# Attention denominators by transposes and a free-dimension sum, with the recurrence's input kept in natural order

## The chip, the cores and the metric

The kernel runs on one core of a Trainium2 chip. The metric is the device time in microseconds (us) of one execution; of several executions the median is given. Five engines work side by side, each with its own queue[...]: PE (TensorE, matrix products; PEld is its weight load), DVE (VectorE), ACT (ScalarE), POOL (GpSimd) and SP (SyncE, which here issues the transfers). On-chip memory is SBUF; matrix products land in PSUM[...]. All data is float32.

## The reference

The input `x` has shape (4, 128, 64, 64): four batches, 128 channels, 4096 positions. Two layers follow each other. Cut to what matters:

```python
# layer 0: every position attends to all others, 64 channels inside
q, k, v = wq @ x, wk @ x, wv @ x                   # per batch, 64 x 4096
x = x + wo @ (softmax(k^T q) applied to v)

# layer 1: t = tokens of x, 4 x 4096 x 128
t = t + causal_attention(layernorm(t), Wq, Wk, Wv)
# layer 1, second half: batch norm over all tokens, then a recurrence in time
Wx = layernorm(t) @ W.T
Wx = (Wx - mean) * rsqrt(var + 1e-5) * gamma + beta
def step(y, wx_t):
    y = sigmoid(wx_t + y @ V.T)
    return y, y
_, ys = scan(step, zeros, Wx over the 4096 time steps)
t = t + ys
```

Each attention needs, for every query, the sum of its exponentials: the softmax denominator. The recurrence is sequential over 4096 steps in the reference.

## The kernel before

The kernel has a fast path and a general one behind a flag that the fast path computes. Only the fast path runs here. Keys lie on partitions and queries along the free dimension, in blocks of 512 queries (`BLK`), so the exponentials `p` are summed over keys in two moves: DVE adds them up elementwise over all key tiles (`dsum`, then `den`, 128 x 512), and the 128 partitions that remain are summed at the end of each block. There are 64 blocks: 2 layers, 4 batches, 8 blocks each.

```python
def project(layer, b, g, agg, den):
    dp = misc("den_ps")                              # one of two shared PSUM buffers
    for j in range(TPB):                             # TPB = 4
        nc.tensor.matmul(dp[:, j : j + 1], lhsT=den[:, ts(j, P)], rhs=ones, start=True, stop=True)
    rec = recs[:, layer, b, ts(g, TPB)]
    nc.vector.reciprocal(rec, dp[:, :TPB])
    op = misc("o_ps")
    for j in range(TPB):
        nc.tensor.matmul(op[:, ts(j, P)], lhsT=agg[:, ts(j, P)], rhs=wv1 if layer else wo2, ...)
    for j in range(TPB):
        t = xs[:, b, ds(g * BLK + j * P, P)]
        nc.vector.scalar_tensor_tensor(t, in0=op[:, ts(j, P)], scalar=rec[:, j : j + 1], in1=t, ...)
```

A product with the one-column `ones` puts the sums of 128 queries on 128 partitions, one per partition, as `rec` is needed there.

The recurrence is cut into `NCH` = 256 chunks of `STEPS` = 16 time steps, which run side by side: one instruction handles one step of all 256 chunks of a batch. Each chunk first runs `WARM` = 12 steps of the chunk ahead of it to reach its starting state; a count at the end compares these states with the true ones and feeds the flag. The input of the recurrence is stored so that the 32 chunks of a block of 512 lie side by side for each step:

```python
# in the last stage of a block of layer 1 (third())
wp = misc("wx_ps")
nc.tensor.matmul(wp, lhsT=wf, rhs=mem["xhT"], start=True, stop=True)
nc.vector.bn_stats(stats[:, b * NB + g], wp)
nc.scalar.copy(
    xs[:, b, ts(g, BLK)].rearrange("p (s c) -> p s c", c=CPB),     # CPB = 32
    wp.rearrange("p (c s) -> p s c", s=STEPS),
)
...
by_step = xs.rearrange("p b (g s c) -> p b s g c", s=STEPS, c=CPB)

def step(b, s):                                      # s from -12 to 15
    wx = by_step[:, b, s % STEPS]
    if s == -1:  y = start[:, b, 1:]
    elif s < 0:  y = yp.tile(...)
    else:        y = wx                              # the result takes the place of its input
    ps = ps_y.tile(...)
    nc.tensor.matmul(ps, lhsT=vf, rhs=prev[b], start=True, stop=True)
    z = yp.tile(...)                                 # the sum goes to SBUF
    nc.vector.scalar_tensor_tensor(z, in0=wx, scalar=scale, in1=ps, op0=ALU.mult, op1=ALU.add)
    nc.scalar.activation(y, z, AF.Sigmoid, bias=shift)
    prev[b] = start[:, b, :NCH] if s == -1 else y

def residual(b):                                     # after the last step of a batch
    for g in range(NB):                              # NB = 8
        engine = nc.vector if g < ON_DVE[b] else nc.gpsimd
        t = xr[:, b, ts(g, BLK)].rearrange("p (c s) -> p c s", s=STEPS)
        y = xs[:, b, ts(g, BLK)].rearrange("p (s c) -> p c s", c=CPB)
        engine.tensor_tensor(t, t, y, ALU.add)
    for h in range(2):
        nc.sync.dma_start(out=out[b, :, half], in_=xr[:, b, half])

ON_DVE = (0, 0, 4, 5)
pace = (1.40, 1.60, 1.75, 1.87)                      # order in which the batches' steps are written
```

`xr` holds the tokens before the recurrence; it is stored to memory as `x2` during the attention and loaded again at its end. The scheduler of the language may move instructions within a queue, so the written order isn't always the one that runs.

Of the kernel before, what the change touches and what calls it, by code (L numbers as in the profile page):

```python
# [9 lines left out]
F32 = mybir.dt.float32  # L10
AF = mybir.ActivationFunctionType
ALU = mybir.AluOpType
AX = mybir.AxisListType
PSUM = bass.MemoryType.PSUM

P = 128
BLK = 512
# [325 lines left out]
def fast_path(  # L343
# [20 lines left out]
    nc = tc.nc  # L364
    B, C, N = x.shape
    M = c_wqT.shape[1]
    assert C == P and M == P // 2 and N % CHUNK == 0
    NT = N // P
    NB = N // BLK
    TPB = BLK // P  # L370
    SHIFT = 32.0
    LOW, HIGH = 1e-25, 1e25
    WARM, TOL, STEPS = 12, 1e-6, 16
    NCH = N // STEPS
    CPB = BLK // STEPS

    const = ctx.enter_context(tc.tile_pool(name="const", bufs=1))
    xpool = ctx.enter_context(tc.tile_pool(name="x", bufs=1))
# [4 lines left out]
    xs = xpool.tile([P, B, N], F32, name="xs")  # L383
# [3 lines left out]
    def load(name, shape, *parts):  # L387
        t = const.tile(shape, F32, name=name)
        for dst, src in parts:
            nc.scalar.dma_start(out=dst(t), in_=src)  # L390
        return t
# [15 lines left out]
    vf = load("vf", [P, P], (whole, f_vT))  # L407
# [3 lines left out]
    ident = const.tile([P, P], F32, name="ident")  # L411
    make_identity(nc, ident)
    ones = const.tile([P, 1], F32, name="ones")
# [17 lines left out]
    with tc.tile_pool(name="batch", bufs=1) as batch, tc.tile_pool(name="rows", bufs=2) as rowp, tc.tile_pool(  # L431
        name="prob", bufs=4
    ) as prob, tc.tile_pool(name="work", bufs=2) as wk, tc.tile_pool(name="stat", bufs=4) as stat, tc.tile_pool(
        name="ps_s", bufs=2, space=PSUM
    ) as ps_s, tc.tile_pool(name="ps_a", bufs=2, space=PSUM) as ps_a, tc.tile_pool(
        name="ps_m", bufs=2, space=PSUM
    ) as ps_m:

        def misc(name):
            return ps_m.tile([P, BLK], F32, tag="m", name=name)  # L440
# [52 lines left out]
        def project(layer, b, g, agg, den):  # L493

            dp = misc("den_ps")
            for j in range(TPB):
                nc.tensor.matmul(dp[:, j : j + 1], lhsT=den[:, ts(j, P)], rhs=ones, start=True, stop=True)  # L497
            rec = recs[:, layer, b, ts(g, TPB)]
            nc.vector.reciprocal(rec, dp[:, :TPB])
            op = misc("o_ps")  # L500
            for j in range(TPB):
                nc.tensor.matmul(  # L502
                    op[:, ts(j, P)], lhsT=agg[:, ts(j, P)], rhs=wv1 if layer else wo2, start=True, stop=True
                )
            for j in range(TPB):
                t = xs[:, b, ds(g * BLK + j * P, P)]
                nc.vector.scalar_tensor_tensor(  # L507
                    t, in0=op[:, ts(j, P)], scalar=rec[:, j : j + 1], in1=t, op0=ALU.mult, op1=ALU.add
                )
# [37 lines left out]
        def finish1(b, g):  # L547
            agg, den = bs[b].agg, bs[b].den
            mem = {}

            def first():
                project(1, b, g, agg, den)
                mem["xh"] = wk.tile([P, TPB, P], F32, tag="xh2", name="xh2")
                normed(b, g, mem["xh"])

            def second():
                t = xs[:, b, ts(g, BLK)].rearrange("p (j c) -> p j c", c=P)
                xc = wk.tile([P, BLK], F32, tag="xc", name="xc")
                transposed(t, xc, "tT_ps", nc.scalar.copy)
                nc.sync.dma_start(out=x2[b, :, ts(g, BLK)], in_=xc)  # L560
                mem["xhT"] = wk.tile([P, BLK], F32, tag="xhT2", name="xhT2")
                transposed(mem["xh"], mem["xhT"], "xh2T_ps", nc.vector.tensor_copy)

            def third():
                wp = misc("wx_ps")
                nc.tensor.matmul(wp, lhsT=wf, rhs=mem["xhT"], start=True, stop=True)  # L566
                nc.vector.bn_stats(stats[:, b * NB + g], wp)

                nc.scalar.copy(
                    xs[:, b, ts(g, BLK)].rearrange("p (s c) -> p s c", c=CPB),  # L570
                    wp.rearrange("p (c s) -> p s c", s=STEPS),
                )

            yield 1, first
            yield 3, second
            yield 1, third
# [15 lines left out]
        for b in range(B):  # L592
            for g in range(NB):
                block(0, b, g, [((t, 0, BLK), (t + NT // 2, 0, BLK)) for t in range(NT // 2)])
            for g in range(NB):
                full = [((t, 0, BLK), (t + 1, 0, BLK)) for t in range(0, TPB * g, 2)]
                d = [(TPB * g + r, r * P, BLK - r * P) for r in range(TPB)]
# [150 lines left out]

    with tc.tile_pool(name="xr", bufs=1) as xrp, tc.tile_pool(name="y", bufs=2) as yp, tc.tile_pool(
        name="ps_y", bufs=2, space=PSUM
    ) as ps_y:
        xr = xrp.tile([P, B, N], F32, name="xr")
        for b in range(B):
            nc.sync.dma_start(out=xr[:, b], in_=x2[b])

        mv = xrp.tile([P, nc.vector.BN_AGGR_DIM], F32, name="mv")
        nc.vector.bn_aggr(mv, stats)
        scale = xrp.tile([P, 1], F32, name="scale")  # L760
        var = xrp.tile([P, 1], F32, name="var")
        nc.vector.tensor_scalar(var, mv[:, 1:2], BN_EPS, None, ALU.add)
        rsqrt(scale, var, xrp.tile([P, 1], F32, name="z"))
        nc.vector.tensor_tensor(scale, scale, gamma, ALU.mult)
        shift = xrp.tile([P, 1], F32, name="shift")
        nc.vector.tensor_tensor(shift, mv[:, 0:1], scale, ALU.mult)
        nc.vector.tensor_tensor(shift, beta, shift, ALU.subtract)

        by_step = xs.rearrange("p b (g s c) -> p b s g c", s=STEPS, c=CPB)
        start = xrp.tile([P, B, NCH + 1], F32, name="start")  # L770
        nc.gpsimd.memset(start[:, :, 0:1], 0.0)
        prev = [None] * B

        def step(b, s):

            grid = lambda t: t.rearrange("p (g c) -> p g c", c=CPB)
            wx = by_step[:, b, s % STEPS]
            if s == -1:
                y = grid(start[:, b, 1:])
            elif s < 0:  # L780
                y = grid(yp.tile([P, NCH], F32, tag=f"y{b}", name="y"))
            else:
                y = wx
            if prev[b] is None:
                nc.scalar.activation(y, wx, AF.Sigmoid, scale=scale, bias=shift)
            else:
                ps = grid(ps_y.tile([P, NCH], F32, tag=f"y{b}", name="y_ps"))
                nc.tensor.matmul(ps, lhsT=vf, rhs=prev[b], start=True, stop=True)  # L788
                z = grid(yp.tile([P, NCH], F32, tag=f"z{b}", name="z"))
                nc.vector.scalar_tensor_tensor(z, in0=wx, scalar=scale, in1=ps, op0=ALU.mult, op1=ALU.add)  # L790
                nc.scalar.activation(y, z, AF.Sigmoid, bias=shift)
            prev[b] = grid(start[:, b, :NCH]) if s == -1 else y

        def residual(b):

            for g in range(NB):
                engine = nc.vector if g < ON_DVE[b] else nc.gpsimd
                t = xr[:, b, ts(g, BLK)].rearrange("p (c s) -> p c s", s=STEPS)
                y = xs[:, b, ts(g, BLK)].rearrange("p (s c) -> p c s", c=CPB)
                engine.tensor_tensor(t, t, y, ALU.add)  # L800
            for h in range(2):
                half = slice(h * N // 2, (h + 1) * N // 2)
                nc.sync.dma_start(out=out[b, :, half], in_=xr[:, b, half])


        ON_DVE = (0, 0, 4, 5)
        pace = (1.40, 1.60, 1.75, 1.87)
        turns = [((s + WARM + 1) * pace[b], b, s) for b in range(B) for s in range(-WARM, STEPS)]
        for _, b, s in sorted(turns):
            step(b, s)  # L810
            if s == STEPS - 1:
                residual(b)


        count = xrp.tile([P, 2], F32, name="count")
        d = xrp.tile([P, B, NCH], F32, name="d")
        for b in range(B):
            grid = lambda t: t.rearrange("p (g c) -> p g c", c=CPB)
            nc.vector.tensor_tensor(grid(d[:, b]), by_step[:, b, STEPS - 1], grid(start[:, b, 1:]), ALU.subtract)
        nc.vector.tensor_tensor(d, d, d, ALU.mult)  # L820
        nc.vector.tensor_scalar(d, d, TOL * TOL, None, ALU.is_le)
        nc.vector.tensor_reduce(count[:, 0:1], d.rearrange("p b c -> p (b c)"), AX.X, ALU.add)

        r = recs.rearrange("p l b t -> p (l b t)")
        r2 = xrp.tile([P, 2 * B * NT], F32, name="r2")
        nc.vector.tensor_scalar(r2, r, LOW, None, ALU.is_ge)
        nc.vector.tensor_scalar(r, r, HIGH, None, ALU.is_le)
        nc.vector.tensor_tensor(r, r, r2, ALU.mult)
        nc.vector.tensor_reduce(count[:, 1:2], r, AX.X, ALU.add)
        total = xrp.tile([P, 1], F32, name="total")  # L830
        nc.vector.tensor_reduce(total, count, AX.X, ALU.add)
        tp = ps_y.tile([1, 1], F32, tag="y0", name="tp")
        nc.tensor.matmul(tp, lhsT=total, rhs=ones, start=True, stop=True)
        nc.vector.tensor_scalar(flag, tp, P * (B * NCH + 2 * B * NT) - 0.5, None, ALU.is_lt)


# [56 lines left out]
```

## Time and profile before

| What | Value |
|---|---|
| Time, median of 3 (lowest to highest) | 2267.13 us (2266.6 to 2267.83) |
| Span of the profiled execution | 2266.1 us |
| Mean granted TensorE clock | 0.987 |
| Recurrence, first activation to last | 2163.1 to 2215.2 us |
| Line 497, one-column products, PE passes | 512 of 246 ns |
| Line 497, weight loads | 512 of 191 ns |
| Line 499, reciprocal on DVE | 64 of 178 ns |
| Line 791, activation of the recurrence | 108 of 508 ns |
| Line 694, DVE add of 128 x 512, both inputs in SBUF | 64 of 692 ns |
| Line 800, residual add of 128 x 512 on POOL | 23 of 1917 ns |
| Line 800, the same on DVE | 9 of 2348 ns |

A row of the profile's groups gives the line, engine, operation, the tiles written and read with their shapes, the count, then busy time and mean duration, and what ended the idle time before it. The duration of an instruction overlaps with its neighbours', so a count times a mean can be more than the time that the engine took. The chain of waits follows the run back from its last instruction and so tells which work set the end.

### The profile page before, as it was taken

What the parts mean: (1) busy time and instruction counts of PE and PEld (TensorE: products, weight loads), DVE (VectorE), ACT (ScalarE), POOL (GpSimd) and SP (SyncE); (2) the same over time, 40 slices, a digit from 0 to 9 for tenths busy, and PEclk for the clock granted to TensorE, in tenths of its full rate; (3) what the DMA queues carried; (4) which work ended last, traced back from release to release, by engine and by line L of the source; (5) the groups of instructions that cost most, each with busy time, mean ns of one, the idle gap of its engine ahead of it and who ended that gap; (6) DMA issues with size and microseconds to landing.
All of it is one profiled execution on the core that took longest, in us unless ns stands there. A gap on an engine that the chain in (4) does not pass through costs nothing.

```text
span 2266.1 us, 31438 instructions
## 1 busy us (share of the span) xinstructions
PE 2185.7 (96%) x12764; PEld 1004.1 (44%) x12764; DVE 1440.8 (64%) x2684; ACT 1013.4 (45%) x1122; POOL 148.7 (7%) x230
## 2 busy tenths in 40 slices
PE   7999999999999999999999999999999999999980
PEld 3434355454333345544343435554434434544450
DVE  4877764444787774544678776444477876544486
ACT  4666623323666543333566552333366653333281
POOL 0000010000000000000000001000000001000007
PEclk9999999999999999999999999999999999999985
DMA  4000000000000000000000000000000000000033
GB/s 158 1 1 1 1 10 10 5 5 5 6 1 1 1 5 10 10 5 5 6 1 1 1 1 10 10 5 5 10 1 1 1 1 5 10 10 5 10 149 150
DMA packets 10536, 36.17 MB, mean 16 GB/s; under 512 B 1936, under 2 KB 2704, under 8 KB 8848
## 3 DMA queue, kind: packets, MB, share of 16 engines
q1 hardware_dynamic: 8640, 33.56, 3.8%
q8 instruction: 102, 1.67, 0.3%
q10 hardware_dynamic: 1744, 0.53, 0.1%
q14 instruction: 50, 0.41, 0.1%
HBM read 17.30 MB, written 16.78 MB: 15 GB/s over the span
## 4 chain that ended last, share of the span: by engine, by line
PE 92%; issue 3%; POOL 2%; DVE 2%; DMA 1%; ACT 0%; ACTq 0%; POOLq 0%; DVEq 0%
PE s_ps L620 20%; PE acc L679 20%; PE s_ps L611 20%; PE acc L671 19%; PE o_ps L502 3%; PE den_ps L497 2%; POOL xr L800 2%; PE r_ps L474 1%; PE wx_ps L566 1%; PE v_ps L469 1%; PE r_ps L488 1%; PE xhT_ps L531 1%; PE kc_ps L461 1%; PE xT_ps L483 1%; PE xh2T_ps L531 1%
## 5 line engine op out<-in xcount | busy, mean ns | idle before, releaser
L651 DVE TENSOR_TENSOR dsum<-dsum,p 128x1024 f32<-128x1024 f32 x676 | 827.7, 1224 | 507.6 <-ACT p L627 336.5
L625 ACT ACTIVATE p<-s_ps,nshift 128x1024 f32<-128x1024 f32 x512 | 570.9, 1115 | 380.2 <-PE s_ps L611 380.1
L627 ACT ACTIVATE p<-s_ps 128x1024 f32<-128x1024 f32 (+2 forms) x288 | 274.2, 952 | 632.6 <-PE s_ps L620 522.1
L611 PE MATMUL s_ps<-rows,kc 64*64 64x512 f32 x4096 | 538.6, 594 | 0.0
L671 PE MATMUL acc<-p,v 64*64 64x512 f32 x4096 | 535.2, 590 | 0.0
L620 PE MATMUL s_ps<-rows,xhT 128*128 128x512 f32 (+3 forms) x1152 | 504.9, 560 | 2.6 <-DVE rows L490 2.6
L679 PE MATMUL acc<-p,xh 128*128 128x512 f32 (+3 forms) x1152 | 501.6, 557 | 0.0
L679 PEld LDWEIGHTS acc<-p,xh 128*128 128x128 f32 x1152 | 215.9, 190 | 243.2 <-issue 234.7
L620 PEld LDWEIGHTS s_ps<-rows,xhT 128*128 128x128 f32 x1152 | 210.6, 190 | 229.0 <-issue 184.5
L671 PEld LDWEIGHTS acc<-p,v 64*64 64x64 f32 x4096 | 159.1, 133 | 279.9 <-issue 273.8
L611 PEld LDWEIGHTS s_ps<-rows,kc 64*64 64x64 f32 x4096 | 146.9, 133 | 248.2 <-issue 233.7
L425 POOL TENSOR_TENSOR ln_rstd<-ln_var,mhalf 128x4 f32<-128x4 f32 x64 | 66.7, 1042 | 1222.3 <-DVE ln_var L519 1211.5
L507 DVE SCALAR_TENSOR_TENSOR xs<-o_ps,recs,xs 128x128 f32<-128x128 f32 x256 | 73.0, 344 | 38.4 <-PE o_ps L502 38.4
L659 DVE TENSOR_TENSOR dsum<-dsum,p 128x256 f32<-128x256 f32 (+1 forms) x120 | 55.9, 496 | 64.2 <-POOL p L631 64.2
L631 POOL TENSOR_SCALAR_AFFINE_SELECT p<-p 128x128 f32<-128x128 f32 x128 | 34.5, 293 | 743.1 <-ACT p L627 743.1
L497 PEld LDWEIGHTS den_ps<-ones,den 128*128 128x128 f32 x512 | 64.6, 191 | 40.5 <-issue 20.5
L649 DVE COPY dsum<-p 128x1024 f32<-128x1024 f32 x60 | 41.4, 690 | 61.7 <-ACT p L627 55.4
L523 DVE TENSOR_SCALAR xh<-xs,ln_mv,ln_rstd 128x128 f32<-128x128 f32 x256 | 71.2, 341 | 1.9
L497 PE MATMUL den_ps<-ones,den 128*128 128x1 f32 x512 | 63.9, 246 | 0.0
L516 DVE BATCH_NORM_STATS2 ln_st<-xs 128x6 f32<-128x128 f32 x256 | 63.4, 269 | 0.0
L426 DVE TENSOR_TENSOR ln_z<-ln_rstd 128x4 f32<-128x4 f32 x64 | 10.5, 163 | 68.7 <-POOL ln_rstd L425 68.7
L790 DVE SCALAR_TENSOR_TENSOR z<-xs,scale,y_ps 128x256 f32<-128x256 f32 x108 | 48.5, 480 | 5.1 <-PE y_ps L788 4.5
(93 smaller groups left out, 1124.6 us busy)
## 6 DMA issues: line engine op xcount, KB each, us to landing
xs<-in_x SPq DMA_DIRECT2D x16, 512.0 KB, 7.8
x<-xc SPq DMA_DIRECT2D x32, 256.0 KB, 2.0
xr<-x SPq DMA_DIRECT2D x4, 2048.0 KB, 14.6
out_x<-xr SPq DMA_DIRECT2D x8, 1024.0 KB, 4.5
wk<-in_c_wkT ACTq DMA_DIRECT2D x2, 32.0 KB, 4.9
wo<-in_c_woT ACTq DMA_DIRECT2D x2, 32.0 KB, 4.3
wqT<-in_a_wqT ACTq DMA_DIRECT2D x1, 64.0 KB, 4.5
wkT<-in_a_wkT ACTq DMA_DIRECT2D x1, 64.0 KB, 5.8
```

The lines of the kernel that those rows point to most:

```text
L425: nc.gpsimd.tensor_tensor(y, var, mhalf[:, : y.shape[-1]], ALU.pow)
L497: nc.tensor.matmul(dp[:, j : j + 1], lhsT=den[:, ts(j, P)], rhs=ones, start=True, stop=True)
L502: nc.tensor.matmul(op[:, ts(j, P)], lhsT=agg[:, ts(j, P)], rhs=wv1 if layer else wo2, start=True, stop=True)
L507: nc.vector.scalar_tensor_tensor(t, in0=op[:, ts(j, P)], scalar=rec[:, j : j + 1], in1=t, op0=ALU.mult, op1=ALU.add)
L523: nc.vector.tensor_scalar(dst[:, j], xs[:, b, ds(g * BLK + j * P, P)], mv[:, j, 0:1], y[:, j : j + 1], ALU.subtract, ALU.mult)
L611: nc.tensor.matmul(ps[c * M : c * M + M, off : off + n], lhsT=bs[it.b].kc[part, ds(t % (NT // 2) * P + c * M, M)], rhs=rows[part], start=True,
L620: nc.tensor.matmul(ps[:, off : off + n], lhsT=lhsT, rhs=rhs, start=True, stop=True)
L625: nc.scalar.activation(it.p[:, :off], ps[:, :off], AF.Exp, bias=nshift)
L627: nc.scalar.activation(it.p[:, :off], ps[:, :off], AF.Exp, scale=float(P) ** -0.5)
L651: nc.vector.tensor_tensor(flat, flat, it.p, ALU.add)
L671: nc.tensor.matmul(bt.acc[r][h * M : h * M + M], lhsT=bt.v[part, t], rhs=it.p[part, o : o + n], start=it.first, stop=it.last,)
L679: nc.tensor.matmul(bt.acc[0][:, q0:], lhsT=bt.xh[:, t], rhs=it.p[:, o : o + n], start=it.first and h == 0, stop=it.last and h == 1,)
```

## The change

There are two parts. In the first, the partition sum of `den` is made by transposing its four 128 x 128 pieces on PE and adding along the free dimension with one DVE reduction. In the second, the recurrence's input is kept in the natural order of time, so a step reads every sixteenth element; the sums are written back to PSUM, from where ACT reads them; each step's result goes to a tile of its own and is added to the residual right after its step, on DVE when the step number divides by three and otherwise on POOL, and each batch's output is stored in one transfer. The first part is meant to replace products[...]; the second lets the residual run beside the recurrence and drops the permuted store.

```diff
             dp = misc("den_ps")
             for j in range(TPB):
-                nc.tensor.matmul(dp[:, j : j + 1], lhsT=den[:, ts(j, P)], rhs=ones, start=True, stop=True)
+                nc.tensor.transpose(dp[:, ts(j, P)], den[:, ts(j, P)], ident)
             rec = recs[:, layer, b, ts(g, TPB)]
-            nc.vector.reciprocal(rec, dp[:, :TPB])
+            nc.vector.tensor_reduce(rec, dp.rearrange("p (j k) -> p j k", k=P), AX.X, ALU.add)
+            nc.vector.reciprocal(rec, rec)
 ...
-                nc.scalar.copy(
-                    xs[:, b, ts(g, BLK)].rearrange("p (s c) -> p s c", c=CPB),
-                    wp.rearrange("p (c s) -> p s c", s=STEPS),
-                )
+                nc.scalar.copy(xs[:, b, ts(g, BLK)], wp)
 ...
-    tc.tile_pool(name="y", bufs=2) as yp
+    tc.tile_pool(name="y", bufs=3) as yp
 ...
-        by_step = xs.rearrange("p b (g s c) -> p b s g c", s=STEPS, c=CPB)
+        by_step = xs.rearrange("p b (c s) -> p b s c", s=STEPS)
+        ends = xrp.tile([P, B, NCH], F32, name="ends")
+        xr_by_step = xr.rearrange("p b (c s) -> p b s c", s=STEPS)
 ...
-                y = wx
+                y = ends[:, b] if s == STEPS - 1 else yp.tile(...)          # condensed
 ...
-                z = grid(yp.tile([P, NCH], F32, tag=f"z{b}", name="z"))
-                nc.vector.scalar_tensor_tensor(z, in0=wx, scalar=scale, in1=ps, op0=ALU.mult, op1=ALU.add)
-                nc.scalar.activation(y, z, AF.Sigmoid, bias=shift)
+                nc.vector.scalar_tensor_tensor(
+                    ps[:, :n], in0=wx, scalar=scale, in1=ps[:, :n], op0=ALU.mult, op1=ALU.add
+                )
+                nc.scalar.activation(y, ps[:, :n], AF.Sigmoid, bias=shift)
+            if s >= 0:
+                t = xr_by_step[:, b, s]
+                (nc.gpsimd if s % 3 else nc.vector).tensor_tensor(t, t, y, ALU.add)
+            if s == STEPS - 1:
+                nc.sync.dma_start(out=out[b], in_=xr[:, b])
-        def residual(b): ...                                                # removed, see above
```

In the warm-up a step now covers the 255 chunks that have one ahead of them (`n` = 255) in place of 256, and the check at the end compares the 255 states accordingly.

More of the change, by code (lines that the diff above doesn't have):

```diff
@@ L374, in fast_path @@
     NCH = N // STEPS
-    CPB = BLK // STEPS
     const = ctx.enter_context(tc.tile_pool(name="const", bufs=1))
@@ L744, in fast_path @@
         assert not waiting and not side
-    with tc.tile_pool(name="xr", bufs=1) as xrp, tc.tile_pool(name="y", bufs=2) as yp, tc.tile_pool(
+    with tc.tile_pool(name="xr", bufs=1) as xrp, tc.tile_pool(name="y", bufs=3) as yp, tc.tile_pool(
         name="ps_y", bufs=2, space=PSUM
@@ L767, in fast_path @@
         nc.vector.tensor_tensor(shift, beta, shift, ALU.subtract)
-        by_step = xs.rearrange("p b (g s c) -> p b s g c", s=STEPS, c=CPB)
-        start = xrp.tile([P, B, NCH + 1], F32, name="start")
+        by_step = xs.rearrange("p b (c s) -> p b s c", s=STEPS)
+        start = xrp.tile([P, B, NCH], F32, name="start")
         nc.gpsimd.memset(start[:, :, 0:1], 0.0)
+        ends = xrp.tile([P, B, NCH], F32, name="ends")
+        xr_by_step = xr.rearrange("p b (c s) -> p b s c", s=STEPS)
         prev = [None] * B
         def step(b, s):
-            grid = lambda t: t.rearrange("p (g c) -> p g c", c=CPB)
-            wx = by_step[:, b, s % STEPS]
+            wx = by_step[:, b, s] if s >= 0 else by_step[:, b, STEPS + s, : NCH - 1]
+            n = wx.shape[-1]
             if s == -1:
-                y = grid(start[:, b, 1:])
+                y = start[:, b, 1:]
             elif s < 0:
-                y = grid(yp.tile([P, NCH], F32, tag=f"y{b}", name="y"))
+                y = yp.tile([P, NCH - 1], F32, tag=f"y{b}", name="y")
+            elif s == STEPS - 1:
+                y = ends[:, b]
             else:
-                y = wx
+                y = yp.tile([P, NCH], F32, tag=f"y{b}", name="y")
             if prev[b] is None:
@@ L786, in step @@
             else:
-                ps = grid(ps_y.tile([P, NCH], F32, tag=f"y{b}", name="y_ps"))
-                nc.tensor.matmul(ps, lhsT=vf, rhs=prev[b], start=True, stop=True)
-                z = grid(yp.tile([P, NCH], F32, tag=f"z{b}", name="z"))
[L790 to L806, printed above, removed]
+                ps = ps_y.tile([P, NCH], F32, tag=f"y{b}", name="y_ps")
+                nc.tensor.matmul(ps[:, :n], lhsT=vf, rhs=prev[b], start=True, stop=True)
+                nc.vector.scalar_tensor_tensor(
+                    ps[:, :n], in0=wx, scalar=scale, in1=ps[:, :n], op0=ALU.mult, op1=ALU.add
+                )
+                nc.scalar.activation(y, ps[:, :n], AF.Sigmoid, bias=shift)
+            prev[b] = start[:, b] if s == -1 else y
+            if s >= 0:
[3 more added lines that the diff above has]
+                nc.sync.dma_start(out=out[b], in_=xr[:, b])
         pace = (1.40, 1.60, 1.75, 1.87)
@@ L810, in fast_path @@
             step(b, s)
-            if s == STEPS - 1:
-                residual(b)
         count = xrp.tile([P, 2], F32, name="count")
[L816 to L819, printed above, removed]
+        d = xrp.tile([P, B, NCH - 1], F32, name="d")
+        nc.vector.tensor_tensor(d, ends[:, :, : NCH - 1], start[:, :, 1:], ALU.subtract)
         nc.vector.tensor_tensor(d, d, d, ALU.mult)
@@ L833, in fast_path @@
         nc.tensor.matmul(tp, lhsT=total, rhs=ones, start=True, stop=True)
-        nc.vector.tensor_scalar(flag, tp, P * (B * NCH + 2 * B * NT) - 0.5, None, ALU.is_lt)
+        nc.vector.tensor_scalar(flag, tp, P * (B * (NCH - 1) + 2 * B * NT) - 0.5, None, ALU.is_lt)
 def kernel(
```

## The prediction

> **What bounds the kernel now.** I read the page first: busy shares, then the chain of waits.
>
> ```profile
> PE 2185.7 (96%) x12764; PEld 1004.1 (44%) x12764; DVE 1440.8 (64%) x2684; ACT 1013.4 (45%) x1122; POOL 148.7 (7%) x230
> ...
> PE 92%; issue 3%; POOL 2%; DVE 2%; DMA 1%; ACT 0%; ACTq 0%; POOLq 0%; DVEq 0%
> ```
>
> Both say TensorE. A busy PE alone proves little, because its ends are modelled; the chain confirms it, since it runs through PE work for 92% of the span. The PE rows of the waits list no wait over 1 us in the attention stage, and the busy table by stretch has PE at 2074.53 of 2080.00 us between 50 and 2130. There a TensorE saving counts in full, and 64% DVE leaves room. The change, though, also touches the last 100 us, where another order holds:
>
> ```profile
> 2190.00:2210.00 20.00, 20.00 (x90) 13.14 (x89) 19.72 (x45) 20.00 (x45) 0.00 (x0) 1.00 0.00 1
> 2210.00:2230.00 20.00, 4.66 (x21) 2.87 (x20) 19.95 (x20) 5.72 (x13) 15.52 (x8) 0.71 0.13 53
> 2230.00:2250.00 20.00, 0.19 (x2) 0.08 (x2) 17.54 (x11) 0.00 (x0) 20.00 (x11) 0.50 0.34 143
> ```
>
> Columns after the length: busy (count) of PE, PEld, DVE, ACT, POOL, then clock, DMA share, GB/s. The reader is to see two regimes: a recurrence (first row) in which POOL does nothing, and a residual stage in which PE and ACT do nothing. The timeline of that tail shows the same; first column start, second length:
>
> ```profile
> 2214.49 43.29 POOL L800 TENSOR_TENSOR xr<-xr,xs 128x512 f32<-128x512 f32 x23 [54.42 <-ACT xs L791]
> ...
> 2216.21 20.50 DVE L800 TENSOR_TENSOR xr<-xr,xs 128x512 f32<-128x512 f32 x9
> 2222.23 35.91 SPq L803 DMA_DIRECT2D out_x<-xr  x8
> ```
>
> So from 2214.5 the end is set by POOL's residual adds (to 2257.8) and then one 1 MB store.
>
> **Stage one, the denominators: what goes.** From the chain in order of time (start, length, what):
>
> ```profile
> 74.55 0.59 PE xhT_ps L531 x4
> ...
> 95.83 0.98 PE den_ps L497 x8
> 96.82 1.00 PE o_ps L502 x8
> 97.81 1.02 PE s_ps L611 x8
> ...
> 315.92 0.44 PE xhT_ps L531 x4
> ...
> 319.79 0.79 PE den_ps L497 x8
> ```
>
> Four products are eight PE passes (float32 goes in two), each with its own 128x128 weight load[...]. They hold the chain 0.98 us per block in layer 0 and 0.79 in layer 1: 32 x 0.98 + 32 x 0.79 = 56.6 us, the 2.5% that the chain gives line 497.
>
> **What comes.** Four transposes are four passes. The kernel already does 128x128 float32 transposes of this form (line 531): 0.59 us for four when they follow 64x64 work as in layer 0, 0.44 in layer 1. New cost 32 x 0.59 + 32 x 0.44 = 33.0 us; saved 23.6 us. A second gain lies in the projection behind it: its 1.00 us is eight 128-column passes, each 0.11 us going by the four transposes (0.44/4), so 0.88, plus 0.12 us for a first load that a one-column product can't hide. Behind a 128-column transpose it may be hidden: up to 64 x 0.12 = 7.7 us. I take some 3 us, so **26.5 us** in all, between 22 and 32.
>
> **DVE's side.** The sum over 128x512 from PSUM should cost about what the 128x512 PSUM copy at line 490 costs, 682 ns, so 64 x 0.7 = 45 us, 64% to 66% of the span. It ends before the four updates at line 507 would start anyway: the projection takes 1.0 us after the transposes, sum plus reciprocal 0.7 + 0.18. I count 0.5 us for late buffers, which leaves 26.
>
> [...] the sum itself isn't in this trace. [...] with POOL running, 128x512 adds on DVE took 2348 ns (line 800) against 692 (line 694), while the recurrence's scalar_tensor_tensor, one input in PSUM, has a maximum of 483 ns, its last ones beside POOL's adds. [...] The new recurrence steps by 64 bytes. No row here isolates that in SBUF; a permuting PSUM read at line 569 took 585 ns like the straight copies. I count no penalty but widen the range.
>
> **Stage two, the recurrence.** Warm-up first:
>
> ```profile
> L790 DVE SCALAR_TENSOR_TENSOR z<-xs,scale,y_ps 128x256 f32<-128x256 f32 x108 | 48.5, 480 | 5.1 <-PE y_ps L788 4.5
> ```
>
> Before, 112 activations ran at one per 20.89/46 = 0.454 us with ACT at 100% (first table above). ACT binds; DVE's 480 ns overlap. The change lets ACT read the sum from PSUM. At line 627 ACT reads PSUM at 490 ns for 384 elements and 0.83 ns per element more, so 384 ns at 256, plus some 92 ns that line 625 (1115) has over 627 (1023) with a bias tile: 476 against 508. Cadence 0.42, saving 0.03 x 48 = 1.5 us. The stretch of 23.6 us (2163.1 to 2186.7) becomes about 22.5.
>
> Then 16 true steps of four batches. Work added to them: 64 residual adds of 128x256, on DVE when the step number divides by three (24), else on POOL (40). POOL's adds of 512 took 1.48 us undisturbed (8.88/6 at the end of the chain), so 256 by about 0.8: 40 x 0.8 = 32 us. A DVE add of 256 is 464 ns at line 659, plus up to one POOL add of waiting, about 1.0 in all. The batches keep step in spite of the paces in the code:
>
> ```profile
> L791 ACT ACTIVATE start<-z,shift x4: 509/509/510, 2184.8 to 2186.2; 128x256 f32<-128x256 f32 x4
> ```
>
> All four last warm steps start within 1.4 us. So residuals come in waves: two rounds of four POOL adds each (2 x 1.8 us of ACT, but 6.4 us of POOL), then a round of four DVE adds that meet POOL still at work. Three rounds: 3.6 us for the first two, and for the third four DVE sums at 0.40 plus four adds at about 0.85, 5.0: 8.6 us. Sixteen rounds: 5 x 8.6 plus 3.3 for the undisturbed first, about **46 us** instead of 28.5.
>
> **The end.** Nothing of the old residual stage (2215 to 2257.8) remains. But four stores of 2 MB each become ready nearly together. The four 2 MB loads of xr, issued back to back, took up to 22.0 us to land (tile view of xr), so the stores should take about 22 from the first issue, 20 from the last residual, plus some 2 us to the end as before.
>
> **Sum.** Recurrence starts at 2163.1 - 26 = 2137; plus 22.5 and 46 is 2205.5; plus 20 and 2 is 2227.5. Batch 0 has priority in program order and may finish early, which overlaps its store: I take 3.5 off for half of that chance, plus 1 us from span to metric: **2225 us**, 42 below.
>
> **Rivals.**
> - **Only TensorE's saving lasts**: POOL's adds with 64-byte steps for both read and write take 1.2 us or more, or DVE's strided reads slow the sums; then the recurrence costs 80 us or more after warm-up, all the 42 us of old residual stage are given back, and the time is 2240 to 2255. For it: DVE's 2348 ns under POOL. Against it: the 483 ns maximum.
> - **Residuals vanish under the recurrence**: POOL at 0.7, DVE adds fall where POOL is idle, and batches spread so that only the last store stands out. Main part 38 us, tail 15: 2205 to 2212. For it: POOL's 0.00 busy in the recurrence.
> - **DVE's sum stalls TensorE** through the two shared PSUM buffers: the saving of 26 falls to 10, time 2240. Against it: the PE rows of the waits put 10 us on DVE in the whole span, the final flag left out.
>
> **Range and chances.** 2205 to 2250 covers the second rival's floor and most of the first. The border of 2% is 2221.8, 3 us under my value, so faster by over 2% has 0.38, within 2% 0.57. Slower needs more than 87 us of error: 0.05.
>
> **What would show it.** Right: line 497 with 256 transposes at 0.44 to 0.59 us a block in the chain; the sum near 0.7 us; the first recurrence activation near 2137; POOL adds near 0.8; DVE adds near 1.0; four stores overlapping for about 20 us. Wrong: DVE sums well over 480 ns (strides), POOL adds over 1.2, PE waiting on den_ps's reader, or the batches ending far apart.

## The result, and the profile after

The changed kernel takes 2232.09 us (median of 4, 2231.04 to 2232.86) against 2267.31 us: ratio 0.9845, 95% interval 0.9828 to 0.9862, so 35.2 us less. Its profiled execution has a span of 2229.1 us. Its lines are numbered anew: 496 to 499 are the denominators, 785 to 792 the recurrence, 796 the residual adds, 798 the stores.

The busy shares and the chain of waits on the page after:

```profile
PE 2169.0 (97%) x12508; PEld 971.6 (44%) x12508; DVE 1484.9 (67%) x2760; ACT 1016.7 (46%) x1122; POOL 142.5 (6%) x247
...
PE 93%; DVE 5%; issue 1%; DMA 0%; ACT 0%; POOL 0%; ACTq 0%; DVEq 0%; POOLq 0%
```

PE still carries the chain. What is new is DVE at 5% where POOL and DVE had 2% each: in the last 90 us the chain runs through another engine now. First the denominators, in the chain in order of time (start, length, what), one block of layer 0 and one of layer 1:

```profile
63.84 0.59 PE den_ps L496 x4
64.43 0.89 PE o_ps L502 x8
65.32 1.02 PE s_ps L607 x8
...
315.40 0.44 PE den_ps L496 x4
315.83 0.89 PE o_ps L502 x8
```

The transposes take the 0.59 and 0.44 us of the older transposes, and the projection behind them went from 1.00 to 0.89 us in both layers. Then the tail, as busy time by stretch (length, then PE, PEld, DVE, ACT, POOL, clock, DMA share, GB/s):

```profile
2136.00:2164.00 28.00, 27.10 (x94) 15.75 (x94) 25.25 (x46) 23.67 (x49) 0.00 (x0) 0.92 0.56 238
2164.00:2217.00 53.00, 36.83 (x123) 18.21 (x122) 50.42 (x88) 30.26 (x64) 36.40 (x40) 0.99 0.22 95
2217.00:2230.00 13.00, 0.19 (x2) 0.09 (x2) 4.38 (x6) 0.00 (x0) 0.00 (x0) 0.50 0.64 268
```

The first row is the warm-up, the second the true steps with their residual adds, the third the last store. In the second, DVE is busy for 50.42 of 53 us, ACT for 30, POOL for 36: the bound has moved from ACT to DVE. In the warm-up too DVE runs without a pause once it has started, here 44 sums in a row (timeline: start, length):

```profile
2140.71 24.40 DVE L789 SCALAR_TENSOR_TENSOR y_ps<-xs,scale,y_ps 128x255 f32<-128x255 f32 x44 [0.20 <-PE y_ps L788]
```

The groups say why:

```profile
L789 DVE SCALAR_TENSOR_TENSOR y_ps<-xs,scale,y_ps 128x256 f32<-128x256 f32 (+1 forms) x108 | 62.5, 658 | 6.0 <-PE y_ps L788 6.0
L792 ACT ACTIVATE y<-y_ps,shift 128x256 f32<-128x256 f32 (+1 forms) x100 | 47.3, 474 | 22.5 <-DVE y_ps L789 16.3
```

DVE's sum of a step takes 658 ns where it took 480, and ACT now waits for it. The first activations, which read the input directly, tell the same (802 ns on average after, 589 before). Here is line 785 in the kernel before, then in the changed one (ns of the shortest, the median and the longest, first and last start):

```profile
L785 ACT ACTIVATE y<-xs,shift,scale x4: 585/586/600, 2163.1 to 2164.5; 128x256 f32<-128x256 f32 x4
L785 ACT ACTIVATE y<-xs,shift,scale x4: 799/800/812, 2136.0 to 2138.2; 128x255 f32<-128x255 f32 x4
```

The stores, from the timeline:

```profile
2201.03 16.19 SPq L798 DMA_DIRECT2D out_x<-xr  x4
```

The first and the last issue lie 16 us apart (2201.0, 2209.4, 2214.3 and 2216.9). A store lands 6.3 us after its issue, the last one after 9.5. So the first two are done and the third is under way when the last residual add ends at 2216.8.

Where the 37.0 us between the two spans lie: the recurrence starts 27.0 us sooner (2136.0 against 2163.1), and from there to the end it is 93.1 us against 103.0, 9.9 less.

### The profile page after: what moved, and what is told of

The parts are those of the page before. It is cut to its first block, busy times and chain, and to the rows that moved or that the text cites. A ratio compares the mean times of both kernels' runs of the same rounds, so it can differ in the third digit from the quotient of the medians.

```text
span 2229.1 us, 31036 instructions
## 1 busy us (share of the span) xinstructions
PE 2169.0 (97%) x12508; PEld 971.6 (44%) x12508; DVE 1484.9 (67%) x2760; ACT 1016.7 (46%) x1122; POOL 142.5 (6%) x247
## 4 chain that ended last, share of the span: by engine, by line
PE 93%; DVE 5%; issue 1%; DMA 0%; ACT 0%; POOL 0%; ACTq 0%; DVEq 0%; POOLq 0%
PE s_ps L616 21%; PE s_ps L607 20%; PE acc L675 20%; PE acc L667 19%; PE o_ps L502 3%; DVE y_ps L789 2%; PE r_ps L473 1%; PE den_ps L496 1%; PE wx_ps L566 1%; PE v_ps L468 1%; PE r_ps L487 1%; PE xhT_ps L531 1%; PE kc_ps L460 1%; PE xT_ps L482 1%; DVE xr L796 1%
## 5 line engine op out<-in xcount | busy, mean ns | idle before, releaser
L788 PE MATMUL y_ps<-y,vf 128*128 128x256 f32 (+1 forms) x208 | 61.9, 436 | 20.9 <-ACT y L792 14.1
L789 DVE SCALAR_TENSOR_TENSOR y_ps<-xs,scale,y_ps 128x256 f32<-128x256 f32 (+1 forms) x108 | 62.5, 658 | 6.0 <-PE y_ps L788 6.0
L792 ACT ACTIVATE y<-y_ps,shift 128x256 f32<-128x256 f32 (+1 forms) x100 | 47.3, 474 | 22.5 <-DVE y_ps L789 16.3
L788 PEld LDWEIGHTS y_ps<-y,vf 128*128 128x128 f32 x208 | 32.8, 194 | 51.0 <-ACT y L792 41.8
```

The source lines that it names most:

```text
L788: nc.tensor.matmul(ps[:, :n], lhsT=vf, rhs=prev[b], start=True, stop=True)
L789: nc.vector.scalar_tensor_tensor(ps[:, :n], in0=wx, scalar=scale, in1=ps[:, :n], op0=ALU.mult, op1=ALU.add)
```

## Experiments

The median of the kernel before differs by up to 0.9 us from chip to chip (2267.31 to 2268.23), so times of kernels that ran on different chips compare to about 1 us.

**The two parts alone.** Does each part bring what its stretch of the trace shows?

```diff
# e1: before, with the denominators of the changed kernel
# e2: the changed kernel, with
-   nc.tensor.transpose(dp[:, ts(j, P)], den[:, ts(j, P)], ident)
-   nc.vector.tensor_reduce(rec, dp.rearrange(...), AX.X, ALU.add)
-   nc.vector.reciprocal(rec, rec)
+   nc.tensor.matmul(dp[:, j : j + 1], lhsT=den[:, ts(j, P)], rhs=ones, ...)
+   nc.vector.reciprocal(rec, dp[:, :TPB])
```

> Only the transposes and the DVE sum; recurrence and residual as before. If the 27 us by which the recurrence starts earlier is this part's whole worth and nothing later gives it back: 2267.3 - 27 = 2240 us (2238 to 2243), first recurrence activation at 2136. Rival, that the earlier start owes something to the contiguous copy of the recurrence input: 2245 or more.

> Only the new recurrence; denominators by one-column products. If the parts are independent: 2232.1 + 27 = 2259 us, so 8 faster than before, with the first activation at 2163 and the recurrence, residual and stores taking 93 us from there. Rival, that the parts help each other: 2265 or more.

Measured: denominators alone 2241.23 us (ratio 0.9882, 0.9866 to 0.9899), 26.6 less than the 2267.86 of before on that chip; recurrence alone 2260.99 (0.9969, 0.9956 to 0.9981), 6.9 less. The sum of 33.5 is within 2 us of the 35.2 of both. To that accuracy the parts are independent, and three quarters of the gain is the denominators'.

**Why the sum takes 650 ns: the step of 64 bytes, or the write to PSUM?** The change brought both. Each experiment keeps one.

```diff
# e3: the changed kernel (step of 64 bytes stays)
-   nc.vector.scalar_tensor_tensor(ps[:, :n], in0=wx, scalar=scale, in1=ps[:, :n], ...)
+   nc.vector.scalar_tensor_tensor(z[:, :n], in0=wx, scalar=scale, in1=ps[:, :n], ...)
# e4: e1 (runs of 32 stay)
-   nc.vector.scalar_tensor_tensor(z, in0=wx, scalar=scale, in1=ps, ...)
+   nc.vector.scalar_tensor_tensor(ps, in0=wx, scalar=scale, in1=ps, ...)
```

> The changed kernel with one thing undone: the sum of a step goes to SBUF again, the input is still read with a step of 64 bytes. Theory stride: the DVE sum still takes about 650 ns, ACT goes back to 508 ns, time within 3 us of 2232. Rival, writing to PSUM: the DVE sum falls to 480 ns, the warm-up from 27.9 to 24 us, and with 64 more sums in the true steps the time to about 2220.

> Denominators as changed, recurrence as before with one thing changed: the sum stays in PSUM, the input lies in runs of 32. Theory stride: DVE sum at about 480 ns, ACT at 474 and binding at 0.42 per activation, recurrence 48 us instead of 52, time about 2236. Rival, writing to PSUM: DVE sum 650 ns, recurrence 62 us, time about 2250.

The groups of e3, then of e4:

```profile
L790 DVE SCALAR_TENSOR_TENSOR z<-xs,scale,y_ps 128x256 f32<-128x256 f32 (+1 forms) x108 | 63.4, 674 | 7.9 <-PE y_ps L788 7.8
```

```profile
L790 DVE SCALAR_TENSOR_TENSOR y_ps<-xs,scale,y_ps 128x256 f32<-128x256 f32 x108 | 48.4, 488 | 4.1 <-PE y_ps L789 4.1
```

With the step and SBUF as target 674 ns, with runs and PSUM as target 488; the kernel before (runs, SBUF) has 480 and the changed one (step, PSUM) 658. So it is the step: it adds 194 ns with SBUF as target and 170 with PSUM. Times: e3 2232.58 (0.9844, 0.9828 to 0.9861), equal to the changed kernel; e4 2239.98 (0.9878, 0.9861 to 0.9894), 1.3 under e1. I had expected e4 at 2236. The activation did fall from 508 to 475 ns, but the whole recurrence, from the first activation to the first residual add, fell only from 51.4 to 50.4 us. The 64 activations of the true steps take 28.59 us, 0.447 each, where e1 has 29.02; the 0.42 that I had worked out doesn't come about. A stretch of e4 (columns as above) shows why:

```profile
2163.50:2183.50 20.00, 20.00 (x91) 13.30 (x90) 20.00 (x45) 19.86 (x46) 0.00 (x0) 1.00 0.00 1
```

DVE is busy for all of the 20 us, so a shorter activation soon meets the sums as the next bound.

**The batches' ends.** In the kernel before the batches ran in step in spite of the order written. Here the last warm steps (`start`) still begin within 1.7 us, but the last steps (`ends`) lie 16.4 us apart:

```profile
L792 ACT ACTIVATE start<-y_ps,shift x4: 473/473/473, 2161.8 to 2163.5; 128x255 f32<-128x255 f32 x4
L792 ACT ACTIVATE ends<-y_ps,shift x4: 474/474/475, 2199.3 to 2215.7; 128x256 f32<-128x256 f32 x4
```

```diff
# e5: the changed kernel
-   pace = (1.40, 1.60, 1.75, 1.87)
+   pace = (1.60, 1.60, 1.60, 1.60)
```

> The changed kernel with the four batches' steps written in equal turns. Theory, that the written order makes the batches end 16 us apart and so hides three of the four stores: all four now end within some 3 us, the four stores (8 MB) take about 21 us from the first of them, time about 2241. Rival, that the order written doesn't matter (it didn't in the kernel before): last activations still 16 us apart, 2232.

Measured: 2241.78 us (0.9883, 0.9866 to 0.9899), 9.7 more than the changed kernel. Its stores in the timeline:

```profile
2215.60 3.07 SPq L798 DMA_DIRECT2D out_x<-xr  x4
```

The four are issued within 3 us and the span ends 25.2 us after the first. The last store is issued only 1.3 us later than in the changed kernel (2218.2 against 2216.9), but from there to the end of the span it is 22.6 us instead of 12.2: nearly the whole loss is the stores that no longer run beside the steps. With this pace the prediction's "about 22 from the first issue" and "some 2 us to the end" nearly came about.

**All residual adds on POOL.** Does POOL's work slow DVE's sums?

```diff
# e7: the changed kernel
-   (nc.gpsimd if s % 3 else nc.vector).tensor_tensor(t, t, y, ALU.add)
+   nc.gpsimd.tensor_tensor(t, t, y, ALU.add)
```

> The changed kernel with all 64 residual adds on POOL. Theory, that POOL's adds take 0.87 us whatever DVE does with one SBUF input, and DVE's sums 0.65 whatever POOL does: POOL binds the true steps at 64 x 0.88 = 56 us plus about 3 of start, 6 more than the 53 now, time about 2237; DVE's sums stay at 650 ns. Rival, that the two block each other even with one SBUF input: sums well over 700 ns, time 2250 or more.

Measured: 2242.55 us (0.9888, 0.9871 to 0.9904), 5.5 above what I expected. Groups and stretch of e7:

```profile
L789 DVE SCALAR_TENSOR_TENSOR y_ps<-xs,scale,y_ps 128x256 f32<-128x256 f32 (+1 forms) x108 | 63.3, 645 | 7.8 <-PE y_ps L788 7.0
```

```profile
2164.00:2217.00 53.00, 38.74 (x125) 18.38 (x124) 48.79 (x65) 30.61 (x65) 51.92 (x64) 0.93 0.04 15
```

POOL is busy for 51.92 of 53 us, and the sums still take 645 ns, no more than the 658 of the changed kernel: these sums, with one input in SBUF and one in PSUM, don't feel POOL. POOL did 64 adds in 52 us, 0.81 each, so the true steps are no longer than with the adds shared. They are 6 us shorter than the 59 that I had counted; the stores more than take that back. With the same paces the batches are in step again to the end:

```profile
L792 ACT ACTIVATE ends<-y_ps,shift x4: 468/474/478, 2204.7 to 2206.3; 128x256 f32<-128x256 f32 x4
```

Their last adds stand together at the end of POOL's queue, the stores are issued within 3.7 us, and from the last issue to the end of the span it is 22.6 us (12.2 in the changed kernel).

**The denominator's sum twice.** Is it off the path?

```diff
# e8: e1
+   for _ in range(2):
        nc.vector.tensor_reduce(rec, dp.rearrange("p (j k) -> p j k", k=P), AX.X, ALU.add)
```

> Only the denominator part, with the DVE sum of 0.68 us done twice in each block, 64 x 0.68 = 44 us more on DVE. Theory, that this sum lies beside TensorE's work except where a batch passes to layer 1 (PE then waits for xh: 3.3 us before, 6.2 with the sum, in 4 places): 2241 + 3 = 2244, that wait at about 9 us. Rival, that DVE is on the path: 2255 or more.

Measured: 2245.27 us (0.9899, 0.9882 to 0.9915), 4.0 above e1, for 44 us more of DVE work. PE's waits for `xh` at line 525 of this kernel went from 6.2 to 8.5 us. So some nine tenths of the sum lie beside PE. Of these waits, 3.3 us stand at the end of the attention, and the kernel before has them too. The rest isn't where the expectation put it, at the passage to layer 1, but where a batch ends its layer 1 and the next one begins its layer 0, three times: 1.0 us each in e1 and 1.7 in e8. The first of them in the timeline of e1, then of e8:

```profile
563.07 1.09 PE L532 MATMUL xh2T_ps<-ident,xh 128*128 128x128 f32 x4 [0.96 <-DVE xh L524]
```

```profile
564.53 1.25 PE L533 MATMUL xh2T_ps<-ident,xh 128*128 128x128 f32 x4 [1.74 <-DVE xh L525]
```

The other 1.7 of the 4.0 us aren't placed.

**The change without the step, and what then binds.** e6 keeps the denominators, the runs of 32 and the results in place; it adds the residual after each step and stores each batch in one transfer.

```diff
# e6: e1
-   for g in range(NB): ...                          # residual after the last step
+   xr_by_step = xr.rearrange("p b (g c s) -> p b s g c", s=STEPS, c=CPB)
+   t = xr_by_step[:, b, s]
+   (nc.gpsimd if s % 3 else nc.vector).tensor_tensor(t, t, by_step[:, b, s], ALU.add)
# e9: e6, sums left in PSUM as in e4
# e10: e6
-   (nc.gpsimd if s % 3 else nc.vector)
+   (nc.gpsimd if s % 4 != 3 else nc.vector)
# e11: e10, the add of step s-1 written after step s
# e12: e10, pace = (1.20, 1.45, 1.70, 1.95)
```

> Denominators as changed; the input in runs of 32 and results in place as before; but the residual is added after each step, on DVE where the step divides by three, and each batch stored in one transfer. Theory, that stride in the DVE sum (650 against 480 ns) and not the residual adds cost the recurrence: warm-up 23.6 us, true steps bound by DVE and POOL at about 40, tail 13 to 20 us, time 2212 to 2218. Rival, that the adds beside the sums cost as much as they save: 2232 or more.

> The combined kernel (runs of 32, residual after each step) with the sum of a step left in PSUM. It differs from the changed kernel now in the stride of the input and in where the results lie. Theory, that of the recurrence's two differences from the changed kernel only the stride counts: 2222 less 1 to 2 us, DVE sum 488 ns, ACT 475. Rival, that the place of the sum matters once DVE binds: 2215 or less, or 2230 or more.

> The combined kernel with the residual adds of four of sixteen steps on DVE in place of six (16 adds on DVE, 48 on POOL). Theory, that the adds on DVE at 0.77 us stand in the way of the sums: 8 x 0.77 = 6 us less on DVE, POOL at 48 x 0.87 = 42 us still under the 48 of the true steps, time 2216 to 2219. Rival, that the batches' own chain of product, sum and activation binds: 2222 as before. Third, POOL becomes the bound: 2225.

> As the one with fewer adds on DVE, but each residual add is written one step of its batch later, so that it has a lower place in the order than the next sum. Theory, that a DVE add holds up sums which are ready: another 2 to 4 us less, 2213 to 2216. Rival, that the order in DVE's queue doesn't change: equal to the former within 1 us.

> The kernel with fewer adds on DVE, with the four batches' steps written further apart (1.20, 1.45, 1.70, 1.95). Theory, that the time is now set by the first store and the 25 us that 8 MB of stores take behind it (24.7 in that kernel, 25.2 with equal paces, 25.1 with all adds on POOL): batch 0 ends some 3 to 5 us sooner, first store near 2190, time 2216 to 2219. Rival, that the last batch's end and its own store set it: that end doesn't come sooner, time 2222 or more.

| Kernel | Time, us | Ratio to before (95%) | First store issued, us | Span, us |
|---|---|---|---|---|
| e6 | 2222.07 | 0.9797 (0.978 to 0.9813) | 2194.8 | 2221.1 |
| e9 | 2222.85 | 0.9799 (0.9783 to 0.9815) | 2193.7 | 2221.5 |
| e10 | 2221.69 | 0.9797 (0.9781 to 0.9813) | 2194.8 | 2219.5 |
| e11 | 2221.91 | 0.9796 (0.9779 to 0.9812) | 2196.0 | 2220.6 |
| e12 | 2220.00 | 0.9792 (0.9775 to 0.9808) | 2193.8 | 2218.5 |

e6 is 10 us under the changed kernel, e9 9 us; with 479 and 487 ns for the sum. So the place of the sum hardly counts here either; e9, meant to be 1 to 2 us under e6, is 0.8 over it, and their ranges overlap. The place of the results (in place here, in a tile of their own in the changed kernel) wasn't tested alone. For e6 I had hoped for 2212 to 2218. The true steps still take 48 us, by the stretch of e6:

```profile
2160.00:2209.00 49.00, 35.12 (x126) 21.00 (x125) 45.07 (x92) 29.76 (x66) 36.83 (x40) 0.94 0.25 104
```

DVE is at 45 of 49, its 24 adds at 772 ns among the sums. e10 takes eight adds off DVE, and the timeline has the last store issued 69.7 us after the first activation instead of 72.0. The time hardly moves, 2221.69 and not 2216 to 2219, because the first store isn't issued sooner (60.5 us after the first activation, 58.1 in e6), and the stores now stand in a row: the last one lands after 14.0 us, where one alone takes 6.3. From the first issue to the end of the span e10 has 24.7 us, e12 24.7, e5 25.2, e7 25.1. And POOL has become the bound of e10's true steps, the third case of its expectation, though the time is the rival's (timeline):

```profile
2159.67 44.27 POOL L800 TENSOR_TENSOR xr<-xr,xs 128x256 f32<-128x256 f32 x48 [28.32 <-ACT xs L792]
```

Its 48 adds follow each other without a gap, 0.92 us apart. e12 tests the row of stores by ending batch 0 sooner. The 24.7 behind the first store came as expected, but the first store was issued only 1 us sooner in absolute time (1.7 counted from the first activation) and not 3 to 5, so 2220.00 and not 2216 to 2219. e12 has the lowest median of all kernels; against e10 the ranges overlap (2219.53 to 2221.96 and 2221.41 to 2222.71), so that last step isn't shown to be more than noise. What keeps batch 0 from running further ahead is left open; POOL's full queue (48 adds in 43.72 us in e12 as well) is a candidate that no run tests alone. e11 shows no gain from the later place of the adds.

## Why the prediction was right, and where it wasn't

The time lay in the range, 7 us above the value of 2225, and within the 2% that had the larger chance. Step by step:

- **Denominators: right.** Predicted 26 us, the recurrence starts 27.0 sooner, e1 gives 26.6. The terms behind it were off in opposite senses. The projection's shortening came whole, 0.11 us in 64 blocks or 7.0 us, where I took 3; that the transposes hide a load there was an estimate of mine, and no run isolates it. With the 23.6 of the transposes that is 30.6. Of the missing 3.6, 2.9 are PE's longer wait for `xh` (6.2 against 3.3), where I counted 0.5 for late buffers; the other 0.7 isn't placed. DVE's sum was predicted at 0.7 and took 683 ns.
- **Warm-up: wrong.** Predicted 22.5 us with ACT as the bound (its own sum, 23.6 less 1.5, is 22.1), measured 28.0 (2136.0 to 2164.0). The step that failed is "I count no penalty but widen the range". I had no row with such a step in SBUF to size it. e3 and e4 size it: 170 to 194 ns on a DVE sum of 256 elements, enough to make DVE the bound. No run tries another step, so why it costs this isn't shown. In the warm-up 44 sums take 24.40 us of the timeline, 0.554 each, against 0.42. A smaller part of the miss is in "ACT binds; DVE's 480 ns overlap": the prediction's own first row has DVE at 19.72 of 20.00 us, so there was next to no room behind ACT. In e4, which has no step of 64 bytes, the warm-up takes 23.0 us (2136.1 to 2159.1). So some 5 us are the step's, and 0.5 DVE's being full already.
- **True steps: the sharing of the adds was near, the bound was not.** Predicted 46, measured 52.8 (2164.0 to 2216.8). The term at fault is the same. The sixteen rounds hold 27.6 us for the 64 steps themselves (ten rounds at 1.8 of ACT, six at 1.6 of DVE) and 18.7 for the DVE adds. In the stretch of 53 us the sums alone keep DVE busy for 37.27 us, 9.7 more; the adds bring its busy time to 50.42, so they hold it for 13 more and gave 5.5 back, and DVE is idle for 2.6. The adds were put at 0.85 to 1.0 and took 723 ns on average (20 of 744 and 4 of 616). POOL's 0.8 was 0.87 by its median. On what POOL does to DVE, from which the prediction estimated a wait of up to one POOL add for each DVE add, its two supports from the trace were weak: hardly more than one sum runs beside POOL's adds there (the last sum starts at 2214.7, POOL's first add at 2214.49), and the 2348 ns of line 800 against 692 of line 694 mix POOL's presence with a read of `xs` in steps of 128 bytes. The better test of the sums is e7: 645 ns beside a full POOL.
- **The end: wrong the other way.** Predicted 18.5 after the last residual (20 + 2 less 3.5), measured 12.3. The lockstep of the kernel before was carried over, but here the last activations lie from 2199.3 to 2215.7. The prediction took only 3.5 us off for the chance of it. e5 shows its worth, 9.7 us. That DVE is the bound isn't enough to undo the lockstep: in the warm-up, where it binds as well, the batches stay within 1.7 us. With every add on POOL (e7) they stay within 1.6 us to the end. Of the runs that add the residual after each step, those with adds in DVE's queue and unequal paces issue their stores over 9 us or more, e5 and e7 within 3.7. Why these adds let the written order take hold isn't shown.
- **Rivals.** The first had "DVE's strided reads slow the sums", the right mechanism, but with 80 us or more after the warm-up and the old residual stage given back. From the end of the warm-up to the end of the span it is 65.1 us (79.4 before), so it wasn't. The second's tail came without its 38 us. Of the third, PE stalled by DVE's sum, 2.9 us came, as waits for `xh`; the rows of PE list no wait for the reader of `den_ps`.

So the errors were -1 at the start, +5.5 in the warm-up, +6.8 in the true steps and -6.2 at the end, which is +5.1 on the span (2229.1 against 2224); 2 more are the profiled execution's distance to the metric (1.9, where I took 1) and to the median of the four (1.0). That the total came out within 7 us is in part luck: 12.3 us of errors one way met 7.2 the other way.

## What to carry to other kernels

Four products with a one-column operand held PE for 0.79 to 0.98 us a block here; where PE is the bound, four transposes at 0.44 to 0.59 us and a reduction on an engine with slack (DVE, 64% busy before) can replace them, and the projection behind got shorter too, from 1.00 to 0.89 us. A layout that drops a permuted store can cost more at its readers: here a step of 64 bytes took a sum from 480 to 658 ns and made DVE the bound of a loop with 108 reads, and a kernel that stores in runs, and keeps the results in place, was 9 to 10 us faster. When work moves under a loop, ask which engine then binds it, how full the next engine already is, and whether the outputs still end spread out: with the four 2 MB stores issued over 16 us, the span ended 12.2 us after the last issue, and 22.6 us after it where they were issued within 3 to 4 us (e5, e7).

## What the runs showed of the hardware that I had not expected

- **A DVE add with both inputs in SBUF took 11.48 us beside POOL's row of adds, and 1.23 us without them.** In e7 the check at the end, an add of 128 x 1020 that takes 1232 ns in the changed kernel, meets POOL's row of residual adds. In the timeline (start, length):

```profile
2206.78 11.48 DVE L809 TENSOR_TENSOR d<-ends,start 128x1020 f32<-128x1020 f32 x1 [0.54 <-ACT ends L792]
```

It takes 11.48 us and ends at 2218.3, 1.1 us after POOL's last add, which is about the time that it takes alone; POOL's adds kept to about 1 us meanwhile. In the prediction I had let such a DVE add wait for one POOL add at most.
- **ACT pays for the step in SBUF as well**: 802 ns for 255 elements at line 785 against 589 for 256 in runs of 32, while its permuted PSUM read at line 569 before (585 ns) cost no more than the straight one after (585 ns at line 568).
- **Float32 transposes of this form pass PE once**: 256 PE instructions for 256 transposes, where 256 one-column products had made 512.
